# The last pair of a Mamba and mixture-of-experts tail: gates applied to the experts' products on tokens

## Chip, cores and metric

The kernel runs on one core of a Trainium2 chip. The metric is the device time of one execution in microseconds (us), as the median of several runs. All durations below are in microseconds unless they are marked otherwise.

## The reference, cut to what matters

The input is 128 images of 128 channels and 256 pixels (16 x 16). Layer 0 normalises, quantises and convolves twice. Layer 1 takes each image as 256 tokens of 128 channels, and adds two things to them: a two-way Mamba block, and a mixture of eight experts of which each token uses two. Only layer 1 is touched by the change:

```python
# Mamba block, once forward and once on reversed tokens (256 inner channels)
y = _ssd(xh, dt, A, Bm, Cm) + xh * D[None, None, :, None]
yg = y.reshape(b, l, D_INNER) * jax.nn.silu(z)
yn = yg * jax.lax.rsqrt(jnp.mean(yg * yg, -1, keepdims=True) + EPS) * norm_w
return yn @ out_proj
...
# experts (8 of them, 2 for each token)
router_probs = jax.nn.softmax(x @ router_w + router_b, axis=-1)
top_p, top_i = jax.lax.top_k(router_probs, K)
top_p = top_p / jnp.sum(top_p, axis=-1, keepdims=True)
expert_out = jnp.einsum('bnd,edc->bnec', x, expert_w) + expert_b
gathered = jnp.take_along_axis(expert_out, top_i[..., None], axis=2)
return jnp.einsum('bnk,bnkc->bnc', top_p, gathered)
...
t = t + _L1_attn_ref(_ln_t(t), ...)
t = t + _L1_ffn_ref(_ln_t(t), ...)
```

A gate is the weight of one expert for one token: zero for six of the eight.

## The kernel before

**Pairs and steps.** After the convolutions the kernel handles the images in 64 pairs, numbered 0 to 63. A pair has 512 tokens. They lie either as four tiles of 128 tokens by 128 channels ("on tokens": a token is a partition), or turned round, with channels as partitions and 512 tokens along the row. The work of a pair is cut into parts (`part_a` to `part_f`), which are generators: each `yield` ends a step. The table `T` gives each step of each part a time, and two pairs make a period of 375 places. All steps are sorted by time and issued in that order, so that each engine's order of instructions is written out by hand by the table. The pairs overlap widely: the last steps of pair 62 lie between those of pair 63.

**Queues.** Every engine works through its instructions in this fixed order, and a waiting instruction holds up all behind it on the same engine. All DMAs are issued by SyncE (SP), also in order. `large(...)` makes a big GpSimd operation wait for the latest small VectorE operation that was marked with `alone(...)`.

**The parts that the change touches**, for pair i, direction d (0 forward, 1 backward) and n (half of the 256 inner channels):

- `part_m` multiplies decay factors by products of B and C on VectorE (L1013 and L1018). `part_y` (from L1022) makes the scan's output for (d, n) in `y_ps` on TensorE (L1032, L1038), adds the D term on VectorE into `yg` (L1044), multiplies by silu(z) on GpSimd (L1048) and squares on ScalarE into `sq` (L1051).
- `part_n` adds the squares of n = 0 and n = 1 on GpSimd (L1057), and `part_r` sums them over the partitions with matmuls into `n_ps` (L1065), copies this (L1071), turns it round (L1073), adds an epsilon on VectorE (L1076) and takes the power -0.5 on GpSimd (L1080). That is `rr`, the scale of each token. `part_o` makes the output projection (L1092) and adds it, scaled by `rr`, to the tokens in `t2` (L1102).
- `part_e` normalises `t2`, turns it into `u2T` (channels as partitions, L1114 and L1117), makes the router's logits (L1121, copied by L1126 and turned round by L1128), and finds the two best experts with some twenty small VectorE operations, one power on GpSimd (L1167) and a reciprocal. The gates `gt` (L1179) are on tokens: [128, 4 tiles, 8 experts]. They are turned round (L1182), copied (L1185) and written to DRAM (`g_d`, L1187).
- `part_p` loads the gates of two experts back from DRAM, broadcast to all 128 partitions (`gb`, 512 KB each, L1193; three buffers), and GpSimd multiplies them by `u2T`, expert by expert (L1197). There are four such loads for a pair.
- `part_f` turns `t2` into the bank `f_ps` (L1204), adds eight matmuls of the experts' weights with the gated inputs (L1209), copies the sum (L1212) and stores it (L1214).

**PSUM.** [...] There are two banks with the tag "x", two with "y" and four with "o" (`bank` and `bank4`).

**The last pair in the table.** The steps of `part_e` of pair 63 stand between places 1322 and 1514, those of `part_f` between 1558 and 1839, and those of `part_p` in between. `part_f` of pair 62 has its transposes at place 1396, its eight matmuls at 1425 to 1507 and its copy at 1512; `part_p` of pair 62 has its last load at 1474 and the products with it at 1486 and 1489.

Of the kernel before, what the change touches and what calls it, by code (L numbers as in the profile page):

```python
# [8 lines left out]
F32 = mybir.dt.float32  # L9
BF16 = mybir.dt.bfloat16  # L10
AF = mybir.ActivationFunctionType
ALU = mybir.AluOpType
# [13 lines left out]
NE = 8  # L26
# [8 lines left out]
def kernel(ctx: ExitStack, tc: tile.TileContext, a: dict):  # L35
# [562 lines left out]
    def large(made):  # L598
        if latest:
            info = mybir.DependencyInfo(mybir.DependencyClass.Sync, mybir.DependencyReason.DATA)  # L600
            tc.add_manual_dep(made.ins, latest.pop().name, info, reason="keep apart")
# [143 lines left out]
    def act(out, in_, func, **more):  # L745
# [4 lines left out]
                nc.scalar.preload_act_table_set(need)  # L750
        nc.scalar.activation(out, in_, func, **more)  # L751

    gps, es, ygs, sqs, rrs, t2s, u2Ts, fps, gbs = {}, {}, {}, {}, {}, {}, {}, {}, {}


# [267 lines left out]
    def part_y(i, d, n):  # L1023

        xc, xt = xcs[i, d], xts[i, d]
        s0, s1 = d, 1 - d
        y_ps = bank(f"y_ps{i}_{d}_{n}", "y").rearrange("p (b l) -> p b l", l=NT)
        for k in range(2):
            e0, e1 = es[i, d, k]
            for q in range(2):  # L1030
                h = 2 * n + q
                nc.tensor.matmul(  # L1032
                    y_ps[64 * q : 64 * q + 64, k, :], xt[:, 2 * k + s0, 64 * h : 64 * h + 64],
                    e0[:, h].rearrange("p t l -> p (t l)"), start=True, stop=False,
                )
            for q in range(2):
                h = 2 * n + q
                nc.tensor.matmul(  # L1038
                    y_ps[64 * q : 64 * q + 64, k, s1 * P : (s1 + 1) * P], xt[:, 2 * k + s1, 64 * h : 64 * h + 64],
                    e1[:, h, :], start=False, stop=True,  # L1040
                )
        yield
        yg = ygs[i, d, n] = pr.tile([P, 2 * NT], F32, name=f"yg{i}_{d}_{n}", tag="yg", bufs=5)
        nc.vector.scalar_tensor_tensor(  # L1044
            yg, xc[:, n, :], dcol[:, d, n : n + 1], y_ps.rearrange("p b l -> p (b l)"), ALU.mult, ALU.add
        )
        yield
        large(nc.gpsimd.tensor_tensor(yg, yg, zs[i, d][:, n, :], ALU.mult))  # L1048
        yield
        sq = sqs[i, d, n] = pr.tile([P, 2 * NT], F32, name=f"sq{i}_{d}_{n}", tag="sq", bufs=4)  # L1050
        nc.scalar.activation(sq, yg, AF.Square)  # L1051
        yield

    def part_n(i, d):

        sq = sqs[i, d, 0]
        large(nc.gpsimd.tensor_tensor(sq, sq, sqs[i, d, 1], ALU.add))  # L1057
        yield

    def part_r(i):  # L1060

        n_ps = bank(f"n_ps{i}", "o")
        for d in range(2):
            for t in range(4):
                nc.tensor.matmul(  # L1065
                    n_ps[32 * t : 32 * t + 32, :P], chosen[:, d], sqs[i, d, 0][:, t * P : (t + 1) * P],
                    start=(d == 0), stop=(d == 1),
                )
        yield
        ns = sm.tile([P, P], F32, name=f"ns{i}", tag="ns", bufs=2)  # L1070
        nc.scalar.activation(ns, n_ps[:, :P], AF.Copy, scale=1.0 / DI)  # L1071
        yield
        nc.tensor.transpose(n_ps[:, P : 2 * P], ns, ident)  # L1073
        yield
        rr = rrs[i] = sm.tile([P, 2, 4], F32, name=f"rr{i}", tag="rr")
        nc.vector.tensor_scalar(  # L1076
            rr, n_ps[:, P : 2 * P].rearrange("p (t c) -> p c t", c=32)[:, :2], EPS, None, ALU.add
        )
        yield
        nc.gpsimd.tensor_tensor(  # L1080
            rr.rearrange("p d t -> p (d t)"), rr.rearrange("p d t -> p (d t)"), mhalf, ALU.pow
        )
        yield
# [24 lines left out]
    def part_e(i):  # L1108

        u2 = pr.tile([P, 4, P], F32, name=f"u2{i}", tag="u", bufs=2)  # L1110
        yield from layernorm(sm, t2s[i], u2, f"b{i}")
        u2_ps = bank4(f"u2_ps{i}", "o")
        for t in range(4):
            nc.tensor.transpose(u2_ps[:, t, :], u2[:, t, :], ident)  # L1114
        yield
        u2T = u2Ts[i] = pr.tile([P, 4 * P], F32, name=f"u2T{i}", tag="u2T", bufs=3)
        nc.scalar.activation(u2T, u2_ps.rearrange("p t l -> p (t l)"), AF.Identity, bias=1.0)  # L1117
        yield
        r_ps = bank(f"rt_ps{i}", "o")
        for t in range(4):  # L1120
            nc.tensor.matmul(  # L1121
                r_ps[32 * t : 32 * t + 32, :P], rw, u2T[:, t * P : (t + 1) * P], start=True, stop=True
            )
        yield
        rts = sm.tile([P, P], F32, name=f"rts{i}", tag="rts", bufs=2)
        nc.scalar.copy(rts, r_ps[:, :P])  # L1126
        yield
        nc.tensor.transpose(r_ps[:, P : 2 * P], rts, ident)  # L1128
        yield

        def small8(nm):
            return sm.tile([P, 4, NE], F32, name=f"{nm}{i}", tag=nm)

        def small1(nm):
            return sm.tile([P, 4], F32, name=f"{nm}{i}", tag=nm)

        def bc_e(ap):
            return ap.unsqueeze(2).to_broadcast([P, 4, NE])

        lg = small8("lg")  # L1140
        gt = gts[i % 2][:, : 4 * NE].rearrange("p (t e) -> p t e", e=NE)
        nc.vector.tensor_copy(lg, r_ps[:, P : 2 * P].rearrange("p (t c) -> p t c", c=32)[:, :, :NE])
        yield
        tops, sels = [], []
        for c in range(2):
            mx, sel, fi = small1(f"mx{c}"), small8(f"sel{c}"), small1(f"fi{c}")
            nc.vector.tensor_reduce(mx, lg, AX.X, ALU.max)
            yield
            alone(nc.vector.tensor_tensor(sel, lg, bc_e(mx), ALU.is_equal))
            yield  # L1150

            alone(nc.vector.tensor_tensor(sel, sel, desc.unsqueeze(1).to_broadcast([P, 4, NE]), ALU.mult))
            yield
            nc.vector.tensor_reduce(fi, sel, AX.X, ALU.max)
            yield
            alone(nc.vector.tensor_tensor(sel, sel, bc_e(fi), ALU.is_equal))
            yield
            if c == 0:
                alone(nc.vector.scalar_tensor_tensor(lg, sel, -BIG, lg, ALU.mult, ALU.add))
                yield  # L1160
            tops.append(mx)
            sels.append(sel)

        e2, g1 = small1("e2"), small1("g1")
        alone(nc.vector.tensor_tensor(e2, tops[1], tops[0], ALU.subtract))
        yield
        nc.gpsimd.tensor_tensor(e2, euler, e2, ALU.pow)  # L1167
        yield
        alone(nc.vector.tensor_scalar(g1, e2, 1.0, None, ALU.add))  # L1169
        yield  # L1170
        nc.vector.reciprocal(g1, g1)  # L1171
        yield
        alone(nc.vector.tensor_tensor(e2, e2, g1, ALU.mult))
        yield
        alone(nc.vector.tensor_tensor(gt, sels[0], bc_e(g1), ALU.mult))
        yield
        alone(nc.vector.tensor_tensor(sels[1], sels[1], bc_e(e2), ALU.mult))
        yield
        alone(nc.vector.tensor_tensor(gt, gt, sels[1], ALU.add))  # L1179
        yield  # L1180
        gt_ps = bank(f"gt_ps{i}", "o")
        nc.tensor.transpose(gt_ps[:, :P], gts[i % 2], ident)  # L1182
        yield
        gT = pr.tile([4 * NE, P], F32, name=f"gT{i}", tag="gT")
        nc.scalar.copy(gT, gt_ps[: 4 * NE, :P])  # L1185
        yield
        nc.sync.dma_start(g_d[i % 4].rearrange("e (t l) -> t e l", l=P), gT)  # L1187
        yield

    def part_p(i, q):  # L1190

        gb = pr.tile([P, 2, 4 * P], F32, name=f"gb{i}_{q}", tag="gb", bufs=3)
        nc.sync.dma_start(gb, g_d[i % 4][2 * q : 2 * q + 2, :].partition_broadcast(P))  # L1193
        yield
        for e in range(2):
            gbs[i, 2 * q + e] = gb[:, e]
            large(nc.gpsimd.tensor_tensor(gb[:, e], gb[:, e], u2Ts[i], ALU.mult))  # L1197
            yield

    def part_f(i):  # L1200

        f_ps = bank(f"f_ps{i}", "y")
        for t in range(4):
            nc.tensor.matmul(  # L1204
                f_ps[:, t * P : (t + 1) * P], t2s[i][:, t, :], ident, start=(t == 0), stop=False, is_transpose=True
            )
        yield
        for e in range(NE):
            nc.tensor.matmul(f_ps, ew[:, e, :], gbs[i, e], start=False, stop=(e == NE - 1))  # L1209
            yield  # L1210
        ob = pr.tile([P, 2, NT], F32, name=f"ob{i}", tag="ob", bufs=1)
        nc.scalar.copy(ob.rearrange("p b s -> p (b s)"), f_ps)  # L1212
        yield
        nc.sync.dma_start(out_c[:, 2 * i : 2 * i + 2, :], ob)  # L1214
        yield
# [116 lines left out]
```

## Time and profile before

| | us |
|---|---|
| median of three runs (2533.92 to 2537.05) | 2536.71 |
| the profiled execution | 2536.24 |
| its span, from the first to the last instruction | 2534.5 |
| pair 63's squares added on GpSimd (L1057), start | 2486.90 |
| pair 63's gates (L1179), start | 2511.12 |
| pair 62's output copied (L1212), start | 2516.42 |
| pair 63's output copied (L1212), start | 2530.59 |
| pair 63's output stored (L1214), issue | 2531.21 |

All places in time count from the start of the span. A line of the profile's timeline gives the start, the duration, the engine (PE is TensorE, PEld its weight loads, DVE VectorE, ACT ScalarE, POOL GpSimd, SPq the queue of SyncE), the line of the kernel, the operation, what it writes and reads, and how many instructions were merged into it. The chain of waits follows the work that ended last back from the end, at each step to what released it. An fp32 matmul appears as two passes, each with its own record.

### The profile page before, as it was taken

What the parts mean: (1) busy time and instruction counts of PE and PEld (TensorE: products, weight loads), DVE (VectorE), ACT (ScalarE), POOL (GpSimd) and SP (SyncE); (2) the same over time, 40 slices, a digit from 0 to 9 for tenths busy, and PEclk for the clock granted to TensorE, in tenths of its full rate; (3) what the DMA queues carried; (4) which work ended last, traced back from release to release, by engine and by line L of the source; (5) the groups of instructions that cost most, each with busy time, mean ns of one, the idle gap of its engine ahead of it and who ended that gap; (6) DMA issues with size and microseconds to landing.
All of it is one profiled execution on the core that took longest, in us unless ns stands there. A gap on an engine that the chain in (4) does not pass through costs nothing.

```text
span 2534.5 us, 49248 instructions
## 1 busy us (share of the span) xinstructions
PE 2415.3 (95%) x15936; PEld 1480.5 (58%) x15936; DVE 2241.5 (88%) x6096; ACT 2174.2 (86%) x4451; POOL 1641.9 (65%) x1732
## 2 busy tenths in 40 slices
PE   0889889999999999999999999999999999999997
PEld 0345456666666666666666666666666666666663
DVE  7887799999999999999999999999999999999883
ACT  6778699989888989888898888898988889888881
POOL 5676036666666666676666666666667666666676
PEclk9999899999999999999999999999999999999998
DMA  9468524434344444434444434444433444443333
GB/s 314 149 230 280 169 53 129 122 122 124 112 121 131 125 121 125 121 114 132 133 122 123 125 111 121 131 125 120 126 121 113 133 133 121 122 124 112 113 118 117
DMA packets 302165, 339.57 MB, mean 134 GB/s; under 512 B 56768, under 2 KB 226752, under 8 KB 301888
## 3 DMA queue, kind: packets, MB, share of 16 engines
q1 hardware_dynamic: 301888, 336.21, 43.4%
q8 instruction: 133, 2.18, 0.3%
q14 instruction: 144, 1.18, 0.2%
HBM read 262.72 MB, written 56.62 MB: 126 GB/s over the span
## 4 chain that ended last, share of the span: by engine, by line
PE 89%; DVE 4%; DMA 3%; ACT 2%; POOL 1%; issue 1%; SPq 0%; DVEq 0%; POOLq 0%; ACTq 0%
PE f_ps L1209 17%; PE x_ps L897 13%; PE y_ps L1032 10%; PE z_ps L940 9%; PE o_ps L1092 9%; PE sg L985 5%; PE xt_ps L952 4%; PE y_ps L1038 4%; PE g_ps L971 4%; PE cv L209 4%; DMA xr<-in_x 2%; PE n_ps L1065 1%; PE f_ps L1204 1%; PE u_ps L1114 1%; PE u_ps L770 1%
## 5 line engine op out<-in xcount | busy, mean ns | idle before, releaser
L1197 POOL TENSOR_TENSOR gb<-gb,u2T 128x512 f32<-128x512 f32 x512 | 641.2, 1276 | 122.2 <-PE y_ps L1038 76.1
L915 DVE SCALAR_TENSOR_TENSOR xc<-x_ps,cw,xc 128x510 f32<-128x510 f32 (+2 forms) x768 | 571.0, 744 | 48.4 <-ACT xc L909 38.9
L1048 POOL TENSOR_TENSOR yg<-yg,z 128x512 f32<-128x512 f32 x256 | 325.8, 1278 | 352.2 <-DVE yg L1044 154.5
L1209 PE MATMUL f_ps<-gb,ew 128*128 128x512 f32 x1024 | 510.1, 602 | 6.3 <-POOL gb L1197 6.2
L897 PE MATMUL x_ps<-uT,wx 128*128 128x512 f32 x768 | 402.7, 606 | 8.1 <-ACT e L751 3.5
L751 ACT ACTIVATE e<-sg 128x512 f32<-128x512 f32 x512 | 299.3, 591 | 49.9 <-PE sg L985 44.4
L751 ACT ACTIVATE e<-e,ends 128x128 f32<-128x128 f32 x1024 | 325.0, 392 | 0.0
L1032 PE MATMUL y_ps<-e,xt 128*64 128x256 f32 x2048 | 317.8, 389 | 0.2 <-DVE yg L1044 0.2
L1013 DVE TENSOR_TENSOR e<-e,g_ps 128x1024 f32<-128x1024 f32 x256 | 311.3, 1216 | 5.5 <-ACT e L751 2.7
L915 DVE SCALAR_TENSOR_TENSOR bc<-x_ps,cw,bc 128x510 f32<-128x510 f32 (+2 forms) x384 | 286.5, 746 | 20.8 <-ACT bc L909 4.9
L1209 PEld LDWEIGHTS f_ps<-gb,ew 128*128 128x128 f32 x1024 | 180.3, 192 | 174.4 <-issue 133.9
L940 PE MATMUL z_ps<-uT,wz 128*128 128x512 f32 x512 | 272.5, 614 | 1.6 <-ACT xc L909 1.0
L909 ACT ACTIVATE xc<-x_ps,cb,cw 128x512 f32<-128x512 f32 x256 | 199.0, 777 | 64.6 <-PE x_ps L897 57.7
L1092 PE MATMUL o_ps<-wo,yg 128*128 128x128 f32 x2048 | 249.9, 275 | 0.2 <-DVE e L1018 0.2
L1092 PEld LDWEIGHTS o_ps<-wo,yg 128*128 128x128 f32 x2048 | 239.1, 192 | 11.1 <-DVE g L1169 8.4
L1044 DVE SCALAR_TENSOR_TENSOR yg<-xc,dcol,y_ps 128x512 f32<-128x512 f32 x256 | 189.5, 740 | 50.1 <-PE y_ps L1038 46.7
L1080 POOL TENSOR_TENSOR rr<-rr,mhalf 128x8 f32<-128x8 f32 x64 | 109.6, 1712 | 161.4 <-DVE g L1171 79.6
L1038 PE MATMUL y_ps<-e,xt 128*64 128x128 f32 x2048 | 199.0, 273 | 0.0
L985 PE MATMUL sg<-rows,cols 128*128 128x256 bf16 x1024 | 191.9, 274 | 5.8 <-ACT e L751 2.8
L1038 PEld LDWEIGHTS y_ps<-e,xt 128*64 128x64 f32 x2048 | 147.0, 137 | 74.1 <-DVE e L1018 0.5
L1032 PEld LDWEIGHTS y_ps<-e,xt 128*64 128x64 f32 x2048 | 118.9, 136 | 101.0 <-issue 54.0
L209 PE MATMUL cv<-hpad,wq 128*128 128x512 bf16 x640 | 163.6, 399 | 12.4 <-DVE hpad L183 12.3
(284 smaller groups left out, 4808.9 us busy)
## 6 DMA issues: line engine op xcount, KB each, us to landing
gb<-gd SPq DMA_DIRECT2D x256, 512.0 KB
e<-cum SPq DMA_DIRECT2D x256, 256.0 KB
xr<-in_x SPq DMA_DIRECT2D x64, 256.0 KB
cc<-bc SPq DMA_DIRECT2D x128, 128.0 KB
out<-ob SPq DMA_DIRECT2D x64, 256.0 KB
y<-yt SPq DMA_DIRECT2D x60, 256.0 KB
yt<-y SPq DMA_DIRECT2D x60, 256.0 KB
o<-o SPq DMA_DIRECT2D x56, 256.0 KB
```

The source lines that it names most:

```text
L751: nc.scalar.activation(out, in_, func, **more)
L897: nc.tensor.matmul(ps, wx[d][:, n * P : (n + 1) * P], uTs[i], start=True, stop=True)
L915: nc.vector.scalar_tensor_tensor(acc[:, :, to], raw[:, :, of], cw[:, d, n, 3 - back : 4 - back], acc[:, :, to], ALU.mult, ALU.add,)
L940: nc.tensor.matmul(ps, wz[:, d, n * P : (n + 1) * P], uTs[i], start=True, stop=True)
L985: nc.tensor.matmul(sg[:, :, of], c_[:, k, d, s, half, :], r_[:, :, d, s, of], start=True, stop=True)
L1013: nc.vector.tensor_tensor(e0.rearrange("p h t l -> p h (t l)"), e0.rearrange("p h t l -> p h (t l)"), gps[i, d, k][:, 0:NT].unsqueeze(1).t ...
L1032: nc.tensor.matmul(y_ps[64 * q : 64 * q + 64, k, :], xt[:, 2 * k + s0, 64 * h : 64 * h + 64], e0[:, h].rearrange("p t l -> p (t l)"), star ...
L1038: nc.tensor.matmul(y_ps[64 * q : 64 * q + 64, k, s1 * P : (s1 + 1) * P], xt[:, 2 * k + s1, 64 * h : 64 * h + 64], e1[:, h, :], start=False ...
L1048: large(nc.gpsimd.tensor_tensor(yg, yg, zs[i, d][:, n, :], ALU.mult))
L1092: nc.tensor.matmul(o_ps[:, (2 * j + d) * P : (2 * j + d + 1) * P], ygs[i, d, n][:, t * P : (t + 1) * P], wo[d][:, n, :], start=(n == 0), s ...
L1197: large(nc.gpsimd.tensor_tensor(gb[:, e], gb[:, e], u2Ts[i], ALU.mult))
L1209: nc.tensor.matmul(f_ps, ew[:, e, :], gbs[i, e], start=False, stop=(e == NE - 1))
```

## The change

It touches only the last pair (i == NP - 1, pair 63); no place in the table `T` moves.

- In `part_y` the product with silu(z) is made by VectorE, without `large`.
- `part_n` issues nothing, and `part_r` runs its matmuls over the squares of both n: 16 matmuls instead of 8, summed in PSUM.
- In `part_e`, behind the transpose of the logits, a new function `outputs` makes the experts' products on tokens for the token tiles 0, 1 and 2: for each tile two matmuls with `u2T`'s 128 tokens as the stationary operand and the weights of four experts (512 columns) as the moving one, into two banks. The power on GpSimd becomes an Exp on ScalarE. The transpose of the gates, its copy and its store to DRAM are left out, and all of `part_p`.
- In `part_f`, a new function `weigh` works for each of the four token tiles. ScalarE multiplies the products of experts 5, 6 and 7 by their gates, GpSimd adds these three up, VectorE adds the products of experts 0 to 4, each multiplied by its gate, to `t2`, and then GpSimd's sum. The products for tile 3 are made behind the first of these steps. Then `t2` is turned round into a bank, copied and stored.

```diff
@@ part_y
-        large(nc.gpsimd.tensor_tensor(yg, yg, zs[i, d][:, n, :], ALU.mult))
+        if i == NP - 1:
+            nc.vector.tensor_tensor(yg, yg, zs[i, d][:, n, :], ALU.mult)
+        else:
+            large(nc.gpsimd.tensor_tensor(yg, yg, zs[i, d][:, n, :], ALU.mult))
@@ part_n
-        large(nc.gpsimd.tensor_tensor(sq, sq, sqs[i, d, 1], ALU.add))
+        if i < NP - 1:
+            large(nc.gpsimd.tensor_tensor(sq, sq, sqs[i, d, 1], ALU.add))
@@ part_r
-        for d in range(2):
+        of = [(d, n) for d in range(2) for n in range(2 if i == NP - 1 else 1)]
+        for d, n in of:
             for t in range(4):
                 nc.tensor.matmul(
-                    n_ps[32 * t : 32 * t + 32, :P], chosen[:, d], sqs[i, d, 0][:, t * P : (t + 1) * P],
-                    start=(d == 0), stop=(d == 1),
+                    n_ps[32 * t : 32 * t + 32, :P], chosen[:, d], sqs[i, d, n][:, t * P : (t + 1) * P],
+                    start=((d, n) == of[0]), stop=((d, n) == of[-1]),
                 )
@@ part_e
         nc.tensor.transpose(r_ps[:, P : 2 * P], rts, ident)
+        if i == NP - 1:
+            for t, tags in enumerate(("xx", "oo", "oo")):
+                outputs(i, t, tags)
         yield
...
-        nc.gpsimd.tensor_tensor(e2, euler, e2, ALU.pow)
+        if i == NP - 1:
+            act(e2, e2, AF.Exp)
+        else:
+            nc.gpsimd.tensor_tensor(e2, euler, e2, ALU.pow)
...
+        if i in LAST:
+            for _ in range(3):
+                yield
+            return
         gt_ps = bank(f"gt_ps{i}", "o")
@@ part_p
+        if i in LAST:
+            for _ in range(3):
+                yield
+            return
@@ new functions
+    def outputs(i, t, tags):
+        for half, tag in enumerate(tags):
+            ps = yps[i, t, half] = bank(f"yp{i}_{t}_{half}", tag)
+            nc.tensor.matmul(
+                ps, u2Ts[i][:, t * P : (t + 1) * P], ew[:, 4 * half : 4 * half + 4, :].rearrange("p e c -> p (e c)"),
+                start=True, stop=True,
+            )
+
+    def weigh(i, t):
+        gt = gts[i % 2][:, : 4 * NE].rearrange("p (t e) -> p t e", e=NE)
+        by_act = pr.tile([P, 2 * NT], F32, name=f"ya{i}_{t}", tag="sq", bufs=4).rearrange("p (n c) -> p n c", c=P)
+        for n in range(3):
+            nc.scalar.activation(
+                by_act[:, n, :], yps[i, t, 1][:, (n + 1) * P : (n + 2) * P], AF.Copy, scale=gt[:, t, n + 5 : n + 6]
+            )
+        for n in range(2):
+            nc.gpsimd.tensor_tensor(by_act[:, 0, :], by_act[:, 0, :], by_act[:, n + 1, :], ALU.add)
+        acc = t2s[i][:, t, :]
+        for e in range(5):
+            nc.vector.scalar_tensor_tensor(
+                acc, yps[i, t, e // 4][:, e % 4 * P : (e % 4 + 1) * P], gt[:, t, e : e + 1], acc, ALU.mult, ALU.add
+            )
+        nc.vector.tensor_tensor(acc, acc, by_act[:, 0, :], ALU.add)
@@ part_f
+        if i in LAST:
+            for t in range(4):
+                weigh(i, t)
+                yield
+                if t == 0:
+                    outputs(i, 3, "xx")
+                yield
+            f_ps = bank4(f"f_ps{i}", "y")
+            for t in range(4):
+                nc.tensor.transpose(f_ps[:, t, :], t2s[i][:, t, :], ident)
+            yield
+            ob = pr.tile([P, 2, NT], F32, name=f"ob{i}", tag="ob", bufs=1)
+            nc.scalar.copy(ob.rearrange("p b s -> p (b s)"), f_ps.rearrange("p t l -> p (t l)"))
+            yield
+            nc.sync.dma_start(out_c[:, 2 * i : 2 * i + 2, :], ob)
+            yield
+            return
         f_ps = bank(f"f_ps{i}", "y")
```

More of the change, by code (lines that the diff above doesn't have):

```diff
@@ L751, in act @@
         nc.scalar.activation(out, in_, func, **more)
+    LAST = (NP - 1,)
+    yps = {}
     gps, es, ygs, sqs, rrs, t2s, u2Ts, fps, gbs = {}, {}, {}, {}, {}, {}, {}, {}, {}
```

## The prediction

> **What bounds the kernel now.** I read the page first, then the chain of waits over the last 50 us, then each engine's timeline there. The page says that TensorE rules the span as a whole:
>
> ```profile
> span 2534.5 us, 49248 instructions
> PE 2415.3 (95%) x15936; PEld 1480.5 (58%) x15936; DVE 2241.5 (88%) x6096; ACT 2174.2 (86%) x4451; POOL 1641.9 (65%) x1732
> ```
>
> But the edit is only in pair 63, the last, whose last stages have no later pair beside them. So the chain at the end counts (start us, us, what):
>
> ```profile
> 2486.90 2.49 POOL sq L1057 x2
> 2489.43 0.66 PE n_ps L1065 x8
> 2490.09 2.00 PE f_ps L1209 x2
> ...
> 2504.13 0.47 PE rt_ps L1128
> 2504.60 0.85 PE f_ps L1204 x4
> ...
> 2509.25 1.00 POOL e L1167
> ...
> 2516.37 5.47 DMA gb<-gd
> 2521.97 3.71 POOL gb L1197 x3
> 2525.73 4.80 PE f_ps L1209 x10
> 2530.59 0.58 ACT ob L1212
> ```
>
> Pair 63's squares wait for GpSimd; its gates are ready at 2511.3 (2511.12 + 0.20, L1179 in the same chain), and from there to the copy of the output at 2530.59 lie 19.3 us: gates to DRAM, four reads back, eight products of 1.25, eight matmuls. Pair 62's end runs inside this. Its last gate load is this one on the queue of SyncE (third column: engine):
>
> ```profile
> 2508.90 0.32 SPq L1193 DMA_DIRECT2D gb<-gd  x1
> 2512.38 0.60 SPq L1187 DMA_DIRECT2D gd<-gT  x1
> 2514.34 2.35 SPq L1193 DMA_DIRECT2D gb<-gd  x3
> 2531.21 0.39 SPq L1214 DMA_DIRECT2D out<-ob  x1
> ```
>
> The reader is to see that 2508.90 is just behind pair 62's first four f_ps passes (2505.25 to 2508.66, half clock): this load waits until e = 0 and 1 have freed their buffer. Everything from 2531.21 to the end at 2534.5 stays. Two more facts, from VectorE's and GpSimd's timelines and from a table of stretches (the columns that matter are TensorE's busy us, the first, and its granted clock, third from the right):
>
> ```profile
> 2480.22 1.08 DVE L1149 TENSOR_TENSOR sel<-lg,mx 128x32 f32<-128x32 f32 x1
> 2477.51 4.96 POOL L1197 TENSOR_TENSOR gb<-gb,u2T 128x512 f32<-128x512 f32 x4
> ...
> 2502.90:2506.30 3.40, 2.83 (x15) 1.86 (x16) 1.49 (x6) 0.40 (x2) 2.81 (x3) 0.51 0.15 53
> 2506.30:2509.70 3.40, 3.40 (x6) 1.33 (x5) 1.35 (x8) 0.00 (x0) 1.72 (x2) 0.50 0.00 0
> 2509.70:2513.10 3.40, 2.76 (x8) 1.14 (x7) 0.93 (x6) 0.25 (x1) 2.23 (x3) 0.99 0.41 154
> ```
>
> A small VectorE operation with two SBUF inputs takes 0.19 alone and 1.08 here, ending with a GpSimd product. And TensorE ran at half clock for 6.8 us just where the change puts six new matmuls.
>
> [...]
>
> **The change, part by part** (times are on the clock of the profiled execution).
>
> *Products with z.* GpSimd loses four of 1.27, VectorE gains four;[...] They stand in front of other VectorE work: the first two before L1013 and L1018 of (d 1, k 0), for which y(1,1) on TensorE waits. GpSimd now starts pair 61's gate products at about 2474.7, so the first product waits for the end of one, to about 2477.2, and is done at 2477.8; L1013 (1.2) follows to 2478.9. The second meets the next gate product: 0.6 if VectorE is first, 1.8 if GpSimd is. L1018 then ends at 2480.1 or 2481.3 instead of 2477.9, and y(1,1), which ended at 2479.1, ends at 2481.4 or 2482.6: this edit costs TensorE 2.3 to 3.5 here. Afterwards TensorE runs through without waiting for GpSimd: transposes 0.8, y(1,0) 1.45, pair 61's four matmuls at 0.86, squares, one more of 0.86.
>
> *Squares.* GpSimd's 2.49 at 2486.90 go; n_ps gets 16 matmuls (32 passes) for 8. The 8 passes of 0.43 make this 1.4 to 1.7. Squares are ready (about 2486.6) before TensorE gets there. From y(1,1)'s end: 0.8 + 1.45 + 3.45 + 1.5 + 0.86 = 8.1, so the transpose of the sums is at 2489.5 or 2490.7, against 2491.9. With its half-clocked matmul of 2.00 gone the shift is 1.2 to 2.4; by the same sum at the input of L1080, 1.4 to 2.7. I take 2.0. Should a low clock eat it, it is 0.5. L1080, both o_ps, the layer norm and the router keep their lengths, so L1128 ends at 2502.4 instead of 2504.4.
>
> *Gates.* The power on GpSimd (1.04 behind a gate product of 1.26) becomes an Exp on ScalarE, about 0.25 (L1185's copy), with no table load since Exp's table is in. The gates are ready near 2507.9. This saves 1.4 more, but it isn't worth anything: as follows, nobody waits for them.
>
> *The six matmuls for token tiles 0 to 2.* They stand on TensorE ahead of pair 62's f_ps. Each is two passes, 0.86 at full clock, 1.71 at half: 5.15 to 10.3 together. With half clock for 4.5 us it is 2.6 of them at half and 3.4 at full: 7.4. So pair 62's transposes begin at 2509.8, e = 0 and 1 end 0.45 + 1.72 later, and its last gate load goes at 2512.2 instead of 2508.9. It lands 3.5 later (bounds: 3.1, when the stretches show its traffic over at 2512.0, and 3.8, from 2514.34 to the product at 2518.16). GpSimd's two products end at 2515.8 + 2.5 = 2518.3 (before 2515.16), and ScalarE's copy for pair 62, which followed by 1.26, is at 2519.55 to 2520.15. This is the point: on ScalarE the first of pair 63's products is queued behind this copy, and GpSimd's sums behind those two products.
>
> *The token tiles.* Gone are one DRAM write, four loads, eight gate products and eight matmuls of pair 63, as long as the 19.3 us. In their place, after 2520.15: ScalarE 3 x about 0.3 (L1071 is 0.28 from PSUM[...]), GpSimd two sums of 128x128, which the trace doesn't show (between 0.20, L616's 128x4, and 1.27; by the line through both about 0.46), then VectorE's sum: 2522.5 with one collision[...]. Tile 0's first four products are hidden before. Tiles 1 to 3 take VectorE five products and a sum each. L1102 of the same form takes 0.34 (0.265 back to back); here each waits for the one before, so 5 x 0.375 + 0.3 = 2.15 (bounds 1.7, as L1102 overlaps, and 2.6, with a collision in each). 2522.5 + 3 x 2.15 = 2529.0. ScalarE, GpSimd and tile 3's two matmuls (free of pair 62 at 2519.6 and of bank "x" at 2521.5) lie beside this. Last transpose and copy's start: 0.5, so 2529.5 against 2530.59.
>
> **Sum.** 1.1 us less. The profiled execution took 2536.24 for its span of 2534.5, half a us under the median 2536.71; 2536.24 - 1.1 = 2535.1. A difference under 0.2% (5 us) is about what a measurement of this kernel cannot tell from no change, so the forecast is "within 0.2%".
>
> **Rivals.** *Faster:* full clock for the six matmuls (2.2 less), VectorE first[...] (0.7), tiles of 1.7 (1.3), the shorter load (0.4): 5.7 us in all, 2530.4 or less. [...] *Pair 62 isn't late:* were its last load not held by the new matmuls, TensorE's eight f_ps matmuls would end at 2509.8 + 0.45 + 6.9 = 2517.2 and 2.4 more were gained: 2532.7. The wait at 2508.90 speaks against it. *Slower:* the new matmuls hold pair 62's load too long: at half clock throughout (10.3, and 2.1 more for the transposes and e = 0 and 1), with a shift of 0.5, the copy of pair 62 comes 6.5 later than reckoned; with a collision in two more tiles (0.4 each) the end is 2535.1 + 6.5 + 0.8 = 2542.4. It decides from six matmuls of about 8.5 on, where the gain of 1.1 is used up. For it: the half clock in 2502.9 to 2509.7[...]. That the change doesn't do what it says is excluded: the order of its instructions on each engine is as told.
>
> **Numbers.** Forecast with the second rival, 0.52; faster, 0.33, as three unknown costs break that way, and single prices of dependent operations are guesses; slower, 0.15. The likeliest case alone spans 2532 to 2539. Over all cases 2528.5 to 2542.
>
> **What would show it.** L1080's input some 2 us earlier relative to before; y(1,1) later; six matmuls of "yp" in about 7 us ahead of pair 62's transposes; SyncE's last gate load about 3 us later; ScalarE idle until pair 62's copy and then a comb of four tiles 2.2 us apart on VectorE. Wrong: gates' end followed at once by ScalarE's products, or pair 62's copy before 2517.

## The result and the profile after

| | before | after |
|---|---|---|
| median, 22 runs each | 2537.05 (2533.92 to 2540.18) | 2532.13 (2528.89 to 2537.76) |
| ratio, with its 95% interval | 1 | 0.9984 (0.9977 to 0.9990) |
| span of the profiled execution | 2534.5 | 2527.2 |

The change makes the kernel faster by 0.16%. By the ratio that is some 4 us (2.5 to 5.8), and the medians differ by 4.9. It is real and, by the ratio, within 0.2%, though the far end of the interval lies just beyond (0.23%). The first lines of the page after show that the sums by engine say nothing about so small a step (columns: busy us, share of the span, instructions):

```profile
span 2527.2 us, 49308 instructions
...
PE 2408.3 (95%) x15951; PEld 1477.9 (58%) x15951; DVE 2247.3 (89%) x6124; ACT 2177.6 (86%) x4463; POOL 1627.5 (64%) x1725
```

Nor may the two spans be subtracted. The last `z_ps` matmul of the program, a stage ahead of everything that the change touches, started at 2453.62 in the profiled execution before and at 2448.73 after, and in the profiled executions of the other kernels below, none of which changes anything ahead of it, anywhere from 2448.7 to 2457.8. Of the 7.3 us between the spans 4.9 were there before the change had begun. So all that follows counts from the start of that matmul, and *tail* is the time from there to the end of the span: 80.89 before, 78.43 after, 2.5 us less.

The chain of waits over the end of the profiled execution after (start us, us, engine, what):

```profile
2478.25 3.63 PE f_ps L1273 x8
2481.88 1.01 PE n_ps L1072 x32
2482.89 1.06 PE f_ps L1273 x2
2483.95 0.11 PE n_ps L1080
...
2495.64 0.47 PE rt_ps L1135
2496.11 7.51 PE yp L1225 x12
2503.62 0.44 PE f_ps L1268 x4
2504.06 5.17 PE f_ps L1273 x12
...
2509.23 2.49 POOL gb L1218 x2
...
2511.76 1.14 PE f_ps L1273 x2
...
2512.97 0.59 ACT ob L1276
2513.56 0.54 ACT ya L1235 x2
...
2516.84 6.59 issue
2523.43 0.59 ACT ob L1261
```

GpSimd is gone from in front of `n_ps`: TensorE runs from pair 61's matmuls through the 32 passes of the squares. From 2496.11 to 2512.97 the chain holds only two kinds of work: pair 63's six matmuls (yp, 12 passes, 7.51) and then pair 62's own end, up to its copy (L1276). The first of pair 63's gate products on ScalarE (L1235) starts at the moment this copy ends. The 6.59 of "issue" hide the token tiles; the timeline shows them, with three of pair 63's products with z (yg, L1051), GpSimd's gate products beside these and the last gate load above them (start, duration, engine, line, operation, count, and in brackets the idle time before and what ended it):

```profile
2471.22 1.19 DVE L1051 TENSOR_TENSOR yg<-yg,z 128x512 f32<-128x512 f32 x1
...
2473.46 0.68 DVE L1051 TENSOR_TENSOR yg<-yg,z 128x512 f32<-128x512 f32 x1
...
2474.99 2.50 POOL L1218 TENSOR_TENSOR gb<-gb,u2T 128x512 f32<-128x512 f32 x2 [1.45 <-DMA gb<-gd]
...
2477.68 0.68 DVE L1051 TENSOR_TENSOR yg<-yg,z 128x512 f32<-128x512 f32 x1
2477.84 1.65 POOL L1218 TENSOR_TENSOR gb<-gb,u2T 128x512 f32<-128x512 f32 x1 [0.36 <-DVE sel L1162]
...
2505.80 0.32 SPq L1214 DMA_DIRECT2D gb<-gd  x1
...
2509.23 2.48 POOL L1218 TENSOR_TENSOR gb<-gb,u2T 128x512 f32<-128x512 f32 x2 [6.26 <-PE f_ps L1273]
...
2513.45 3.38 ACT L1235 ACTIVATE ya<-yp,gt 128x128 f32<-128x128 f32 x12
...
2514.38 0.35 DVE L1242 SCALAR_TENSOR_TENSOR t<-yp,gt,t 128x128 f32<-128x128 f32 x1 [11.14 <-ACT ya L1235]
...
2515.63 1.98 DVE L1242 SCALAR_TENSOR_TENSOR t<-yp,gt,t 128x128 f32<-128x128 f32 x5
...
2517.72 0.41 DVE L1245 TENSOR_TENSOR t<-t,ya 128x128 f32<-128x128 f32 x1
2518.12 1.99 DVE L1242 SCALAR_TENSOR_TENSOR t<-yp,gt,t 128x128 f32<-128x128 f32 x5
```

The last gate load went at 2505.80, and the product that needs it started 3.43 later. The timeline puts this wait down to TensorE, whose matmul ended at the same moment (2504.06 + 5.17 = 2509.23); the product waits for the load as well, and in the second profile of the same kernel, below, the same wait is put down to it. VectorE stood still for 11.14 us until ScalarE had done its three products of token tile 0; then tiles follow at a pitch of 2.3 to 2.4.

### The profile page after: what moved, and what is told of

Its sections match the earlier page's. It is cut to its first block, busy times and chain, and to the rows that moved or that the text cites. A ratio compares the mean times of both kernels' runs of the same rounds, so it can differ in the third digit from the quotient of the medians.

```text
span 2527.2 us, 49308 instructions
## 1 busy us (share of the span) xinstructions
PE 2408.3 (95%) x15951; PEld 1477.9 (58%) x15951; DVE 2247.3 (89%) x6124; ACT 2177.6 (86%) x4463; POOL 1627.5 (64%) x1725
## 3 DMA queue, kind: packets, MB, share of 16 engines
q14 instruction: 145, 1.19, 0.2%
## 4 chain that ended last, share of the span: by engine, by line
PE 90%; DVE 3%; DMA 3%; ACT 2%; issue 1%; SPq 0%; POOL 0%; DVEq 0%; ACTq 0%; POOLq 0%
PE f_ps L1273 17%; PE x_ps L899 13%; PE y_ps L1034 10%; PE z_ps L942 9%; PE o_ps L1099 9%; PE sg L987 5%; PE xt_ps L954 4%; PE y_ps L1040 4%; PE g_ps L973 4%; PE cv L209 4%; DMA xr<-in_x 2%; PE n_ps L1072 1%; PE f_ps L1268 1%; PE u_ps L1121 1%; PE u_ps L772 1%
## 5 line engine op out<-in xcount | busy, mean ns | idle before, releaser
L1218 POOL TENSOR_TENSOR gb<-gb,u2T 128x512 f32<-128x512 f32 x504 | 632.3, 1279 | 132.3 <-DMA gb<-gd 45.4
L1273 PE MATMUL f_ps<-gb,ew 128*128 128x512 f32 x1008 | 497.2, 596 | 1.5 <-POOL gb L1218 1.3
L1034 PE MATMUL y_ps<-e,xt 128*64 128x256 f32 x2048 | 317.7, 389 | 1.1 <-PE rt_ps L1128 0.9
L1015 DVE TENSOR_TENSOR e<-e,g_ps 128x1024 f32<-128x1024 f32 x256 | 311.4, 1216 | 6.0 <-ACT e L751 2.4
L1034 PEld LDWEIGHTS y_ps<-e,xt 128*64 128x64 f32 x2048 | 118.9, 136 | 101.8 <-issue 53.6
L1020 DVE TENSOR_TENSOR e<-e,g_ps 128x512 f32<-128x512 f32 x256 | 174.0, 680 | 0.0
```

The lines of the kernel that those rows point to most:

```text
L1015: nc.vector.tensor_tensor(e0.rearrange("p h t l -> p h (t l)"), e0.rearrange("p h t l -> p h (t l)"), gps[i, d, k][:, 0:NT].unsqueeze(1).t ...
L1034: nc.tensor.matmul(y_ps[64 * q : 64 * q + 64, k, :], xt[:, 2 * k + s0, 64 * h : 64 * h + 64], e0[:, h].rearrange("p t l -> p (t l)"), star ...
```

## The experiments

Diffs are against the kernel after, unless another is named. The table has the moments that matter, in us from the start of the last `z_ps` matmul: pair 63's last transpose of router logits ends; the six matmuls end; pair 62's last gate load is issued; the copies of the outputs of pairs 62 and 63 start; the end. The second place is empty where a kernel has no such six matmuls.

| kernel | router | six matmuls | last load | copy 62 | copy 63 | tail |
|---|---|---|---|---|---|---|
| before | 50.99 | | 55.28 | 62.80 | 76.98 | 80.89 |
| before_again | 51.00 | | 55.30 | 62.77 | 77.20 | 81.11 |
| after | 47.38 | 54.89 | 57.08 | 64.24 | 74.70 | 78.43 |
| change_again | 46.75 | 53.08 | 55.27 | 62.88 | 73.33 | 77.07 |
| products_and_squares | 48.37 | | 52.53 | 60.05 | 73.59 | 77.50 |
| squares_only | 47.46 | | 51.76 | 59.26 | 73.69 | 78.27 |
| products_only | 49.24 | | 53.12 | 61.40 | 76.39 | 80.94 |
| gates_only | 50.88 | 58.59 | 60.78 | 67.97 | 78.32 | 82.06 |
| power_on_gpsimd | 48.40 | 55.60 | 57.78 | 64.95 | 75.40 | 79.14 |
| matmuls_behind | 48.05 | 57.41 | 52.30 | 62.65 | 73.09 | 76.83 |
| tiles_ahead | 47.99 | 55.20 | 57.39 | 65.00 | 65.48 | 69.50 |
| tiles_and_matmuls | 49.87 | 58.69 | 53.57 | 65.64 | 67.24 | 70.98 |
| tiles_matmuls_squares | 47.42 | 57.33 | 51.72 | 64.28 | 64.76 | 68.78 |
| tiles_squares | 47.42 | 53.67 | 55.85 | 63.40 | 63.89 | 67.91 |

**How far a tail repeats: before_again, change_again.** Both kernels unchanged, profiled once more.

> The kernel before once more, for how far its tail repeats: 80.9 us in the first look. If the tails can be compared to within a microsecond, 80.0 to 81.8. Rival: the half clock falls elsewhere in the tail and moves it by more than 1.5 us.

> The changed kernel as it is, a second look. Tail 78.4 if the race of VectorE and GpSimd[...] and the clock windows fall as before, up to 79.3 if they fall as in the look with the power on GpSimd.

Before came back at 81.11, 0.2 from its first profile. After came back at 77.07, 1.4 below its own. The chain of waits of change_again shows where:

```profile
2501.10 6.33 PE yp L1225 x12
...
2509.62 3.74 DMA gb<-gd
...
2517.24 0.58 ACT ob L1276
...
2527.68 0.58 ACT ob L1261
```

The six matmuls took 6.33 here for 7.51. The mean clock granted over them was 0.82 here and 0.69 in the first profile: the half clock lasted one window of 3.4 us here, which ended 2.2 us into the six, and two windows there, which ended 4.6 us into them. The router was 0.6 earlier as well (46.75 for 47.38), and from the last load to pair 62's copy it took 0.45 longer. So two executions of one program differ by a window of the clock, and what stands behind moves with it. With only these two profiles, a difference of less than 1.4 us in the tail isn't read where the six matmuls are present.

**The two halves: products_and_squares, gates_only.** One keeps the products with z and the squares and leaves the gates in DRAM, the other the reverse.

```diff
-    LAST = (NP - 1,)
+    LAST = ()
...
-            for t, tags in enumerate(("xx", "oo", "oo")):
-                outputs(i, t, tags)
...
+        nc.gpsimd.tensor_tensor(e2, euler, e2, ALU.pow)
```
```diff
+        large(nc.gpsimd.tensor_tensor(yg, yg, zs[i, d][:, n, :], ALU.mult))
...
+        large(nc.gpsimd.tensor_tensor(sq, sq, sqs[i, d, 1], ALU.add))
...
+        of = [(d, n) for d in range(2) for n in range(1)]
```

> Only the products with z and the squares are moved; the gates and the experts stay as before. I measure the tail in the profile: from the start of the last z_ps matmul to the end of the span (80.9 us before, 78.5 after the change). Theory: these two moves give 3.6 us, and the gates on tokens give a part back, so the tail is 77.3 (3.6 under before), shorter than with the whole change. Rival: the gain comes from the gates on tokens and the earlier squares are hidden behind other waits; then the tail is 80.9 and the time that of before.

> Only the gates are moved to tokens; products with z and squares stay on GpSimd. Theory: six new matmuls ahead of pair 62's last gate load make this about 1.2 us longer than before, a tail of 82.1. Rival: the gates on tokens carry the gain, a tail of 78.5 or less.

Medians over 14 and 13 runs: 2532.02, ratio 0.9984 (0.9976 to 0.9992), and 2536.76, ratio 1.0000 (0.9992 to 1.0008). Tails: 77.50, 3.4 less than before, and 82.06, 1.2 more. Products and squares alone gain as much as the whole change; the gates on tokens, the largest part of the diff, bring nothing by themselves. The chain of the kernel with the gates alone shows why:

```profile
2502.76 7.72 PE yp L1221 x12
...
2519.85 0.58 ACT ob L1272
2520.44 0.54 ACT ya L1231 x2
...
2530.21 0.58 ACT ob L1257
```

The six matmuls put pair 62's copy 5.2 us later than before (67.97 for 62.80), and from this copy's end to pair 63's copy lie 9.8 us of token tiles (2520.43 to 2530.21). In the kernel before the same distance was 13.6 (63.39 to 76.98). 5.2 lost, 3.8 won.

**Which of the two: squares_only, products_only.** Each is products_and_squares with the other edit undone.

> Only the squares are summed by TensorE; products with z stay on GpSimd, gates as before. Theory: each of the two moves alone takes away most of the same wait, because afterwards TensorE's own row of matmuls is next, so they don't add up: a tail of 78.2 (2.7 under before's 80.9; both moves together gave 77.5). Rival: they add up, and this one gives its 2.5 us of GpSimd or about half of the 3.4: a tail of 79.2.

> Only the products with z go to VectorE; the squares are still added by GpSimd, gates as before. Theory, as for the squares alone: a tail of 78.0. Rival: half of the gain, a tail of 79.2.

The squares alone gave 2.6 of the 3.4 by the tail (78.27), and the products alone nothing (80.94); both theories were wrong about the products. But in these two profiles 4.6 us passed between the start of pair 63's copy and the end, for 3.9 before and in products_and_squares, though none of the edits touches anything there. By the start of the copy, the squares alone gave 3.3 of the 3.4 (73.69, against 76.98 before and 73.59 with both) and the products alone 0.6 (76.39). A table of stretches of products_only (TensorE's busy us first, then PEld, DVE, ACT, POOL, the granted clock third from the right):

```profile
2477.96:2481.37 3.41, 1.22 (x18) 0.74 (x15) 3.41 (x4) 1.87 (x4) 1.60 (x2) 1.00 0.80 294
2481.37:2484.79 3.42, 3.39 (x18) 1.85 (x19) 1.34 (x3) 0.63 (x1) 2.80 (x2) 0.50 0.03 9
2484.79:2488.20 3.41, 3.41 (x25) 2.01 (x24) 3.12 (x11) 0.63 (x1) 1.66 (x1) 1.00 0.00 0
```

and its timeline at the start of that:

```profile
2478.41 1.70 DVE L1051 TENSOR_TENSOR yg<-yg,z 128x512 f32<-128x512 f32 x1
...
2480.03 1.21 DVE L1015 TENSOR_TENSOR e<-e,g_ps 128x1024 f32<-128x1024 f32 x1
...
2481.35 1.12 PE L1034 MATMUL y_ps<-e,xt 128*64 128x256 f32 x4 [1.46 <-issue]
```

VectorE has no idle moment in the first row: its product with z takes 1.70, held by two gate products on GpSimd, which end at 2479.56 (2477.07 + 2.49), and L1015, for which y(1,1) waits, stands behind it. TensorE waits 1.46 and is busy for only 1.22 us of that window; the next one runs at half clock. So the last y (y(1,0), the last y_ps matmul of pair 63) ended at 30.92 instead of 27.82, and the sum of the squares on GpSimd still followed. With the squares on TensorE too, the last y ended between 29.04 and 30.39, once at 32.13, against 27.8 wherever the products stayed on GpSimd; but TensorE then need not wait for a product on GpSimd. In the chain of squares_only this wait is seen:

```profile
2486.97 1.28 POOL yg L1050
...
2488.27 0.64 ACT sq L1053
...
2488.95 0.65 PE n_ps L1069 x16
```

The two cancel, or nearly: the output projection (`o_ps`) ended at 39.05 to 39.11 in the three kernels with the squares alone on TensorE, at 39.01 and 38.53 in the two profiles of the whole change, and at 39.47 to 41.73 in the five other kernels that move the products too. What makes the difference is in part the clock: half clock was granted from about 25 us on, amid these y_ps matmuls, in four of the eight profiles with the products on VectorE and in none of the six without. In tiles_and_matmuls, one of the four, four passes of `y_ps` (L1034) took 0.43 ahead of it and 0.85 in it.

**The gates' readiness: power_on_gpsimd.** The Exp on ScalarE becomes the power on GpSimd again.

```diff
-            act(e2, e2, AF.Exp)
+        nc.gpsimd.tensor_tensor(e2, euler, e2, ALU.pow)
```

> The whole change, but the gates' power stays on GpSimd. The gates come 1.4 to 2.5 us later. Theory: nobody waits for them, the tail stays at 78.5 within 0.3. Rival: the gates are on the path, and the tail grows by as much, to 80 or 81.

Tail 79.14, outside the 78.5 within 0.3 that was expected. The gates were ready at 54.98, 2.1 later than in the kernel after (52.90). But the router was already 1.0 late (48.40 for 47.38), after a last y at 30.39 for 29.52; the six matmuls, the load and pair 62's copy followed 0.7 late, and so did the end. Nothing was added behind the gates, which are ready 10 to 11 us ahead of pair 62's copy in both kernels: nothing on the path to the end waits for them.

**The place of the token tiles: tiles_ahead.** The steps of `weigh` for tiles 0 to 2 go ahead of pair 62's last gate products (place 1486) and copy, the one for tile 3 between its last product and its copy; the output gets a buffer of its own.

```diff
@@ part_f
             for t in range(4):
-                weigh(i, t)
-                yield
-                if t == 0:
+                if t == 3:
                     outputs(i, 3, "xx")
+                    yield
+                weigh(i, t)
                 yield
...
-            ob = pr.tile([P, 2, NT], F32, name=f"ob{i}", tag="ob", bufs=1)
+            ob = pr.tile([P, 2 * NT], F32, name=f"ob{i}", tag="yg", bufs=5)
@@ the list of steps
+    EARLY = [1483, 1484, 1485, 1494, 1495, 1508, 1513, 1591]
+            if i in LAST and name == "f":
+                places = [None, EARLY]
```

> The whole change, with the steps of the token tiles moved ahead of pair 62's last gate products on GpSimd and of pair 62's copy on ScalarE, and the output of pair 63 in a buffer of its own. Theory: the change loses its gain by the places of these steps in the queues behind pair 62; ahead of it they fit into idle time, pair 63 ends with pair 62, and the tail is 69.3 (9.2 under the change's). Rival: pair 62's end or the rate of VectorE's products bounds the tail whatever the places, and it stays above 76.

Median 2524.88 over 5 runs, ratio 0.9950 (0.9937 to 0.9963); tail 69.50. The timeline:

```profile
2508.85 2.59 ACT L1235 ACTIVATE ya<-yp,gt 128x128 f32<-128x128 f32 x9 [2.16 <-PE yp L1225]
...
2510.04 2.87 POOL L1239 TENSOR_TENSOR ya<-ya 128x128 f32<-128x128 f32 x6
...
2512.64 0.32 SPq L1214 DMA_DIRECT2D gb<-gd  x1
...
2520.25 0.58 ACT L1276 COPY ob<-f_ps 128x512 f32<-128x512 f32 x1 [1.57 <-issue]
2520.73 0.59 ACT L1261 COPY ob<-f_ps 128x512 f32<-128x512 f32 x1
```

Nine of the twelve products on ScalarE and six of the eight sums on GpSimd run while TensorE is still at the last of the six matmuls and at pair 62's; the last of these sums ends at 2512.91, just after the last gate load is issued. The copies of both pairs follow one another. This one move is worth 8.9 us of the tail (7.6 against change_again), and the two ratios say the same, 0.9950 for 0.9984: what the change had gained was waiting in two queues, on ScalarE behind a copy, on GpSimd behind two products. What each queue and the output's own buffer give by themselves, no run shows.

**The place of the six matmuls: matmuls_behind.** They go behind pair 62's transposes and its experts 0 and 1, so that the gate load isn't held; the tiles stay where the change puts them.

```diff
@@ part_e
-            for t, tags in enumerate(("xx", "oo", "oo")):
-                outputs(i, t, tags)
@@ part_f
+            for t, tags in enumerate(("xx", "oo", "oo")):
+                outputs(i, t, tags)
+            yield
@@ the list of steps
+            if i in LAST and name == "f":
+                places = [None, [1429] + places[1]]
```

> The whole change, but the six matmuls for token tiles 0 to 2 stand behind pair 62's first two f_ps matmuls (e = 0 and 1) instead of ahead of its transposes. Pair 62's last gate load should go about 5 us earlier (at 52 in place of 57.1, from the start of the last z_ps matmul). Theory: the load is no longer what holds pair 62, but TensorE then has the six and the rest of pair 62's matmuls in one row, so pair 62's copy comes only 2.1 earlier: a tail of 76.3. Rival: the load alone decides, the copy follows it by 7.5 at 59.4, and the tail is 73.6. A third: nothing changes, 78.4.

Median 2530.74 over 6 runs, ratio 0.9969 (0.9956 to 0.9981); tail 76.83. The chain:

```profile
2498.08 0.85 PE f_ps L1268 x4
2498.94 3.36 PE f_ps L1273 x4
2502.30 5.15 PE yp L1222 x12
2507.45 5.16 PE f_ps L1273 x12
...
2512.68 0.58 ACT ob L1276
```

The load left at 52.30, 4.8 earlier than in the change, but pair 62's copy came only 1.6 earlier: the same matmuls now stand as one row without a gap from 2498.08 to 2512.61, and TensorE took the place of the load. Its 14.5 us are in the change too (7.51 + 0.44 + 5.17 + 1.14 = 14.3 in the chain of after), only with a wait in them. Against change_again the copy came only 0.2 earlier, and the intervals of the two ratios overlap: a gain over the change isn't shown.

**Both places: tiles_and_matmuls, tiles_matmuls_squares, tiles_squares.** The first joins the last two edits, but with tiles 1 and 2 at places 1490 and 1491: on ScalarE they stay ahead of pair 62's copy, and on GpSimd they stand behind pair 62's last gate products (1486 and 1489), where only tile 0 is ahead of them. The second also leaves the products with z on GpSimd; the third has the tiles and the matmuls as in tiles_ahead and the products on GpSimd.

> Both repairs at once: the gate products of pair 63's tokens ahead of pair 62's last gate product and copy, and its six matmuls behind pair 62's first gate transposes. If two queue places are what held the change back (the tokens' tiles behind pair 62's copy, and the matmuls ahead of the last gate load), then the tail (from the start of the last z_ps matmul to the end of the span) is 68.4 us (69.5 with the tiles alone, 76.8 with the matmuls alone): after the tiles' repair only TensorE's row stands between, so the matmuls' repair is worth about 1 us and not the 1.6 that it gave alone. Rival: the tiles' repair has left TensorE's row of matmuls as the only bound, and it has the same matmuls in any order: tail 69.5 again. Median 2523.5 to 2525 either way, ratio 0.9945.

> The same, with the products with z left on GpSimd and only the squares on TensorE. If the products' move is worth nothing, as the run with it alone says: tail within 0.5 us of that of the kernel with both repairs and the move (68.4), 68.0 to 68.9. Rival: with the end now bound by TensorE, the output projection that starts up to 0.5 us sooner or later decides: 0.8 us longer, 69.2. Median 2523.5 to 2525.

> The gate products of pair 63's tokens ahead of pair 62's last gate product and copy, the six matmuls where the change puts them, and the products with z left on GpSimd. From the router's last transposes to the end of the span it took 21.5 us with the tiles' repair and 21.4 with both repairs (and no move of the products), so moving the matmuls adds 0.1 to 0.4 at most; the router's transposes end 47.4 us after the start of the last z_ps matmul wherever the products stay on GpSimd. Theory (the matmuls' repair is worth nothing once the tiles are repaired): tail 47.4 + 21.5 = 68.9, within 0.3. Rival (the matmuls' repair is worth a microsecond, hidden by the delayed router in the first run with both): 69.8 or more. Ratio 0.994 to 0.995 either way.

Medians over 5 runs each: 2526.79, ratio 0.9951 (0.9938 to 0.9965); 2523.99, ratio 0.9939 (0.9925 to 0.9952); 2523.55, ratio 0.9932 (0.9918 to 0.9945). The first was a miss: tail 70.98 for 68.4, of which 1.9 is a router at 49.87 for 47.99. There two windows of half clock, 6.8 us from 25.49 on, fell on the y_ps matmuls behind the products with z, and the last y ended at 32.13. The second came at 68.78, in the range of its expectation, but this range was drawn around the 68.4 that the first had missed: without the products' move the tail is 2.2 shorter, while the intervals of the two ratios overlap. From the router to the end it is 21.1 with both moves and 21.5 with the tiles' alone; without the products' move 21.4 and 20.5. So these profiles show no gain from the six matmuls' move once the tiles are ahead; as tiles 1 and 2 changed their places with it, its worth alone isn't measured. That tiles_squares came a microsecond under its expectation is the clock again: its six matmuls took 6.46 from their first start to their end (7.42 in tiles_ahead), with one half-clocked window for two. The chain at its end:

```profile
2503.49 6.25 PE yp L1222 x12
2509.74 0.44 PE f_ps L1265 x4
2510.18 1.73 PE f_ps L1270 x4
...
2511.93 3.62 DMA gb<-gd
```

What bounds it now is pair 62's last gate load behind those matmuls. It has the lowest ratio of the case, but its interval overlaps those of the other two, so which of the three is best stays open, and tiles_ahead (0.9937 to 0.9963) overlaps with it too; all of them are faster than the change, whose interval ends at 0.9977.

## Why the prediction came out right, step by step

The forecast was 1.1 us less, inside 0.2%; the ratio gave about 4 and the medians 4.9, at the fast edge of its likeliest case (2532.13, in 2532 to 2539). So the forecast "within 0.2%" was met with little room, and the size was too small. The mechanism held: part of the gain upstream is given back by the six matmuls ahead of pair 62's last gate load, and ScalarE's and GpSimd's queues pass pair 62's lateness on. The terms:

- *Shift of the layer norm and the router, 2.0 taken (1.4 to 2.7).* This term was mis-sized: 3.6 in the first profile (50.99 to 47.38), 4.2 in change_again. The row behind y(1,1) was right as a sum: 8.05 from its end (2475.90) to the transpose at 2483.95, against 8.1. Its terms were off both ways, which was luck: the 32 passes of n_ps took 1.01 for 1.5, pair 61's matmuls 3.63 + 1.06 for 3.45 + 0.86. But y(1,1) ended only 1.7 later (27.17 against 25.48), not 2.3 to 3.5. VectorE's first product was held for less long than reckoned (1.19, done at 2472.41; on the clock of before that is 0.5 earlier than 2477.8), and the second took 0.68 because no gate product stood against it: GpSimd was waiting for a gate load, until 2474.99. The 0.6 reckoned for a product was the author's estimate: not held up, these products took 0.68 to 0.69 (L1051), and L1018, of the same size, takes 0.68 in the profile of before. The squares alone give a shift of 3.5, so the products' move brings nothing that these runs can tell.
- *The six matmuls, 7.4.* 7.51 and 6.33 behind the router, by the chains. The 4.5 us of half clock in this term were taken without a working; 4.6 and 2.2 were met, so that the first fits is luck in part.
- *Pair 62's last gate load 3.3 later, its copy 3.1 later.* 1.8 and 0.0 later for the load, 1.4 and 0.1 for the copy: the sign is the sum's in the first profile, and in the second hardly anything is left. The difference is for the most part the shift, which was 1.6 and 2.2 larger, and in change_again the matmuls, 1.1 shorter than taken. From the load to the product 3.43 (3.5 taken).
- *Gates earlier, worth nothing.* Right: power_on_gpsimd made them 2.1 later, and nothing was added behind them. The Exp took 0.20 (2499.37) for the 0.25 reckoned, and no table load stands with it: ScalarE's last ACT_TABLE_LOAD in the profile after is at 2449.97, 1.28 long.
- *Sums on GpSimd, 0.46 by a line through two sizes.* 0.46.
- *Token tiles.* From pair 62's copy's end to pair 63's copy 9.87, against 9.35 by the prediction's times (2519.55 + 0.6 to 2529.5): the pitch is 2.3 to 2.4 and not 2.15, because the five products take 1.98 and not 1.88, and VectorE's sum 0.29 to 0.41. ScalarE's products, 0.3 each as an estimate, took 0.28 (twelve in 3.38).
- *Pair 63's copy 1.1 earlier.* 2.3 and 3.7 earlier. In the first profile the larger shift gave 1.6 more than reckoned, and the slower tiles took 0.5 of it back.

Of the rivals, "pair 62 isn't late" was priced at 2.4 more; matmuls_behind made it so and its tail was 1.6 shorter (0.2 against change_again), as pair 62's matmuls then stand behind the six all the same. The fast rival (its sum makes 2530.5, not 2530.4) met its conditions by halves: the second product with z wasn't held, but the six matmuls had half clock for 2.2 to 4.6 us, and the tiles were slower. The slow rival needed six matmuls of 8.5 or more; they took 6.3 to 7.5, and the shift was 3.6 or more, not 0.5. One sign that the prediction named against itself, pair 62's copy before 2517 (63.38 from the z_ps matmul), did come in change_again (62.88). It came by the larger shift and the shorter matmuls and not by another path: there too the chain goes through the six matmuls and the last gate load to this copy.

What the prediction saw as "the point" and didn't follow up is where the largest gain lay: once the queue places are named, moving them is worth 7.6 to 8.9 us, more than the whole change.

## What to carry to other kernels

When work of the last stage is taken off a long route (here DRAM and back), look at what its replacement is queued behind on each engine: the shorter route is worth only what the queue places allow, and moving those may be worth more than the route. A load that waits for a buffer is delayed by everything put ahead of the work that frees it (here pair 62's went 1.8 later behind the six matmuls, and 4.8 earlier than that with them moved). And a difference of a few us between two spans is read from the last untouched stage on, not from the start.

## What the runs showed of the hardware

- *VectorE and GpSimd hold each other up.* A 128x512 product of 0.68 on VectorE took 1.19 (after, 2471.22) and 1.70 (products_only, 2478.41) when it met a running GpSimd product, and a GpSimd product of 1.27 took 1.65 (after, 2477.84) when VectorE was first. The loser isn't fixed: in each of these cases it is the one that started later.
- *One program, different clock.* The same six matmuls of the same kernel had half clock for 4.6 us in one execution (after) and for 2.2 in another (change_again). In the tail of before half clock was granted for 3.42 us from 2489.28, 6.82 from 2502.94, 3.42 from 2520.00 and again from 2533.66 on, in that of after for 6.82 from 2493.89 and again from 2517.78 on. The windows of 3.41 us at full clock ahead of these six had TensorE busy, as the profile models it, for 0.83, 1.31, 0.72, 0.27, 1.68 and 1.31, and the one in products_only for 1.22; windows with 2.15 (before, 2523.42) and with 1.97 and 2.07 (after, 2469.99 and 2507.54) were followed by full clock. At half clock, one with 2.88 (before, 2502.94) and two with 2.34 and 0.95 (after, 2493.89 and 2517.78) were followed by half clock again, and those with 3.27, 3.41 and 2.90 (before), 3.41 (after) and 3.39 (products_only) by full. So what the prediction expects of the clock, 4.5 us at half in one case and none in another, is the author's estimate; what grants the clock isn't shown beyond these figures.
- *Two readers of one tile.* In after the fifth product of token tile 0, at 2514.38, stood 11.14 us until ScalarE had done its three products, which read the same tile in PSUM. The four products before it, from the other tile, were long done, and nothing behind it on VectorE ran meanwhile. Most of this wait is ScalarE's own, behind pair 62's copy.
